# Latent attention on one core: joining and scaling the outputs of two head groups by transfers instead of vector transposes

## Chip, core and metric

The kernel runs on one core of a Trainium2 chip. A core has a matrix engine (TensorE, PE in the profile, with its weight loads as PEld), a vector engine (VectorE, DVE), an engine for functions of one operand (ScalarE, ACT), a general engine (GpSimd, POOL) and a queue engine (SyncE, SP) that issues most of the memory transfers (DMAs). Each works through its own instructions in order and they meet at semaphores. The metric is device time in microseconds for one launch; lower is better. Three runs of the kernel before gave 3230.88, 3235.45 and 3238.08 us, so the time before is their median, 3235.45 us.

## What is computed

The input is x, 8 batches of 1024 tokens of 256 numbers in float32. Two residual blocks follow each other: a latent attention, and two layers of local attention with an MLP. The change touches only the first. Cut to what matters:

```
x = x + attn(layernorm(x))                 # the part touched
x = x + two_local_layers(layernorm(x))

attn(x):                                   # 16 heads of 16, causal
    c_kv   = x @ W_kv_down
    k_rope = rotary(c_kv @ W_k_rope);  q_rope = rotary(x @ W_q_rope)
    k = c_kv @ W_k_up;  v = c_kv @ W_v_up;  q = x @ W_q
    scores = (q.k per head + q_rope.k_rope shared) / sqrt(48)
    w = softmax(causal(scores))
    return concat_heads(w @ v) @ W_o
```

## The kernel before

The first part, `mla`, works batch by batch; the second, `local`, follows when all are done. What is told here is `mla`.

**Units and steps.** Keys lie on the 128 partitions and queries run along the free dimension, so a tile of scores is transposed and its exponentials can go straight into the product with v. The 16 heads form four groups `g` of four, the 1024 queries two halves `c` of 512, the keys eight blocks `kb` of 128. A batch is a list of 36 units, made in the loop over `c in (1, 0)` and `g in (0, 2)`: the second half first, two groups at a time, and within such a pair of groups all key blocks, those above the diagonal left out and the short ones joined so that a unit is always 512 columns wide. So units 0 to 12 belong to groups 0 and 1 of half 1, units 13 to 25 to groups 2 and 3 of half 1, units 26 to 30 to groups 0 and 1 of half 0, and units 31 to 35 to groups 2 and 3 of half 0. A pair of groups is called by its half and its number below, (1,0), (1,1), (0,0) and (0,1).

One unit is handled in one step of a software pipeline three steps deep. In step s, `scores` forms the scores of unit s on PE (two tiles of two PSUM banks) and their exponentials on ACT; `turned` multiplies unit s-1's exponentials, two tiles `pt` of 128x1024, on DVE with the exponentials of the rotary scores `er`, which all heads share; `values` multiplies unit s-2's product with v on PE into an accumulator `acc` of one PSUM bank per group. The values of the last two units of a pair of groups are thus formed two steps after the unit, in the steps given in the section on the change.

**The row sums.** A head's v has 17 columns in memory: its 16 and one of ones. `values` takes 32 columns per head as weights, so of the 32 output partitions that a head has in `acc`, the first 16 are its output, the next one is the sum of its softmax row, and the rest is of no use.

**Normalising and joining.** The output product wants the outputs divided by their row sums and wants two groups side by side, 8 heads of 16 on 128 partitions. When a group's last unit is done, ACT copies `acc` to `oaT` (line 503). One step later `finished` (line 507) lets DVE transpose it in blocks of 32x32, so that the tokens come to the partitions and the row sums to a column, forms the reciprocals, and multiplies 16 of each 32 columns into the tile of the even group. One step later still `turn_back` (line 522) transposes the joined tile back once for each pair of groups, into `oT`. The list at the end of each step (lines 654 to 661) carries this.

**Filler.** The projections, rotary scores, normalisations and output products of this batch, the one before and the next are laid beside the steps by a table written out by hand (lines 554 to 591): `(step, which batch, method, arguments)`, where -1 is the batch before and 1 the next. `out_add` forms two tiles of 128 tokens of the output product in a PSUM bank `psx`; the addition to x and the DMA to memory (`x2d`) are owed, and are paid in the middle of the next step's `turned` by `settle`. PSUM has eight banks: four for scores, two for `acc`, and two that all filler shares (`bank`).

**Order.** For PE, DVE, ACT and POOL the order of instructions is that of the program (`manual_schedule`, line 624). SyncE's issues are placed by the framework. It issues the loads of x, the stores of `x2d`, and the placements of q and k: `place_q` and `place_k` copy each freshly made half of q and k from partition order by heads to the layout that `scores` reads. The last batch has no next one: from step 18 on it runs without filler, its own output products are held back to the end, and the first loads and table scalings of `local` come in beside it. After it the loop runs 11 more steps for what is owed.

Of the kernel before, what the change touches and what calls it, by code (L numbers as in the profile page):

```python
# [29 lines left out]
F32 = mybir.dt.float32  # L30
# [52 lines left out]
def preln_mla_local_kernel(  # L83
# [72 lines left out]
    def mla(ctx: ExitStack, verdict):  # L156
# [94 lines left out]

        ers = [late.tile([P, 1280 + 2048 * c], F32, name=f"er{c}") for c in range(2)]

        norms = wp.tile([P, B], F32, name="norms")
        ones = wp.tile([P, 32], F32, name="ones_m")
        nc.gpsimd.memset(ones, 1.0)
# [9 lines left out]
        class Batch:  # L266
# [177 lines left out]

            def start(self):
                b = self.b
                self.rs = small.tile([P, 2, 4, 16], F32, tag="rs", name=f"rs{b}")
                self.acc, self.onat, self.oTs, self.adds = {}, {}, {}, {}

            def scores(self, key, parts):  # L450

# [34 lines left out]
            def values(self, parts, pts):  # L486

                lo, ended = 0, []
                for c, g, kb in parts:
                    q0, w, _ = self.block(c, kb)  # L490
                    if kb == 0:
                        self.acc[g] = pacc.tile([P, 512], F32, tag=f"acc{g % 2}", name=f"acc{self.b}_{c}_{g}")
                    for n in range(4):
                        h = 4 * g + n
                        nc.tensor.matmul(  # L495
                            self.acc[g][32 * n : 32 * n + 32, q0 - c * 512 :],
                            self.v[:, kb, h * VW : h * VW + 32], pts[n // 2][:, n % 2, lo : lo + w],
                            start=(kb == 0), stop=(kb == 4 * c + 3),
                        )
# [7 lines left out]
            def finished(self, c, g, oT):  # L507


                nat = late.tile([P, 16, 32], F32, tag="onat", name=f"onat{self.b}_{c}_{g}", bufs=2)  # L510
                nc.vector.transpose(nat.rearrange("p b d -> p (b d)"), oT)
                r = self.rs[:, c, g]
                nc.vector.reciprocal(r, nat[:, :, HD])
                e = g % 2
                if e == 0:
                    self.onat[c, g // 2] = nat
                nc.vector.tensor_tensor(
                    self.onat[c, g // 2][:, :, HD * e : HD * e + HD], nat[:, :, :HD],
                    r.unsqueeze(2).to_broadcast([P, 16, HD]), ALU.mult,
                )  # L520

            def turn_back(self, c, g):
                if g % 2:
                    t = late.tile([P, 512], F32, tag="oT", name=f"oT{self.b}_{c}_{g}", bufs=3)
                    nc.vector.transpose(t, self.onat.pop((c, g // 2)).rearrange("p b d -> p (b d)"))
                    self.oTs[c, g // 2] = t
                if (c, g) == (0, 3):
                    verdict(self.rs.rearrange("p c g b -> p (c g b)"), f"a{self.b}")

            def out_add(self, t, i, c=None):  # L530

# [20 lines left out]
            beside.setdefault(step, []).append((who, name, args))  # L552

        for step, who, *what in (
            (0, -1, "out_add", 6, 1, 1), (0, 0, "query", 1, 1, 0),
            (1, 0, "query", 1, 1, 1),
            (2, 0, "value", 2), (2, 0, "low"),
            (3, 0, "keys", 1, 0), (3, 1, "normalise", 0, 0),
            (4, 0, "query", 0, 0, 0), (4, 0, "low"), (4, 1, "normalise", 0, 1), (4, 1, "statistics", 1, 0),
            (5, 0, "query", 0, 0, 1), (5, 1, "normalise", 0, 2), (5, 1, "statistics", 1, 1),  # L560
            (6, -1, "out_add", 0, 0), (6, -1, "out_add", 0, 1), (6, 0, "low"), (6, 1, "normalise", 0, 3),
            (7, 0, "query", 1, 0, 0), (7, 1, "normalise", 1, 0),
            (8, 0, "query", 1, 0, 1), (8, 1, "normalise", 1, 1),
            (9, 0, "value", 3), (9, 0, "low"), (9, 1, "normalise", 1, 2),
            (10, -1, "out_add", 2, 0), (10, -1, "out_add", 2, 1), (10, 1, "normalise", 1, 3),
            (11, 0, "keys", 1, 1),
            (12, 1, "turn", 0, 0), (12, 0, "low"),
            (13, 0, "rotary", 0, 2), (13, 1, "turn", 0, 1),
            (14, 1, "down", 0, 0), (14, 0, "rotary", 0, 3),
            (15, 1, "down", 0, 1), (15, 1, "turn", 1, 0),  # L570
            (16, 0, "rotary", 0, 0), (16, 1, "turn", 1, 1),
            (17, 1, "down", 1, 0), (17, 0, "rotary", 0, 1),
            (18, 1, "down", 1, 1), (18, 1, "rope_q", 0, 0, 0),
            (19, 1, "rope_q", 0, 0, 1), (19, 1, "rope_q", 0, 1),
            (20, 1, "rope_k", 0), (20, 1, "rope_q", 1, 0, 0), (20, 2, "load"),
            (21, 1, "rope_q", 1, 0, 1), (21, 1, "rope_q", 1, 1),
            (22, 1, "rope_k", 1), (22, 1, "query", 0, 1, 0),
            (23, 1, "query", 0, 1, 1), (23, 1, "squares", 0),
            (24, 1, "value", 0), (24, 1, "low"), (24, 1, "squares", 1), (24, 2, "statistics", 0, 0),
            (25, 1, "keys", 0, 0), (25, 2, "statistics", 0, 1),  # L580
            (26, 1, "value", 1), (26, 1, "low"),
            (27, 1, "keys", 0, 1), (27, 1, "rotary", 1, 7),
            (28, 1, "rotary", 1, 0), (28, 1, "low"),
            (29, 1, "rotary", 1, 1), (29, 1, "rotary", 1, 6),
            (30, 1, "reach"),
            (31, 0, "out_add", 4, 0), (31, 0, "out_add", 4, 1),
            (32, 1, "rotary", 1, 3),
            (33, 1, "rotary", 1, 2),
            (34, 1, "rotary", 1, 4), (34, 1, "rotary", 1, 5),
            (35, 0, "out_add", 6, 0), (35, 0, "out_add", 6, 1, 0),  # L590
        ):
            at(step, who, *what)

# [29 lines left out]
        line, done, turning = [], [], []  # L623
        with tc.manual_schedule(engines={E.PE, E.DVE, E.Activation, E.Pool}):
            for b in range(B + 1):
                for step in range(len(units) if b < B else 11):
# [36 lines left out]
        ok = small.tile([P, B], F32, tag="okr", name="okr", bufs=1)  # L663
        nc.vector.tensor_scalar(ok, norms, math.log(TURN) / SCALE, None, ALU.is_le)
# [1242 lines left out]
```

## Time and profile before

One profiled execution took 3236.72 us; its span, first to last instruction, was 3235.0 us. Tables are in us.

| what | value |
|---|---|
| median of three runs | 3235.45 |
| profiled execution | 3236.72 |
| its span | 3235.0 |
| PE busy in the span | 3152.4 (97%) |
| DVE busy | 2654.7 (82%) |
| ACT busy | 1734.6 (54%) |
| POOL busy | 1357.5 (42%) |
| granted PE clock, mean | 0.993 |

A share over the whole span says little, since the two parts have different limits. By stretches of the span the same profile has:

| stretch, us | PE busy | DVE busy | ACT busy | DMA share |
|---|---|---|---|---|
| 400 to 520 (`mla`) | 119.19 of 120 | 114.24 | 105.36 | 0.33 |
| 880 to 1000 (end of `mla`, start of `local`) | 91.34 of 120 | 96.17 | 49.25 | 0.35 |
| 1200 to 3235 (`local`) | 2020.13 of 2035 | 1586.38 | 862.15 | 0.47 |

The profile is read with three kinds of lines. A window line gives the busy time of each engine in a stretch. A line of the chain of waits gives start, length and work of one piece of the chain that ended last, followed back from release to release: time saved in a piece of the chain can shorten the run, time saved elsewhere only makes an idle engine idler. A line of a group gives, for one kind of instruction, its source line, engine, operands, count, busy time and mean length, and behind the last bar the idle time before it. PE's instructions overlap and their ends are modelled, so a busy PE is not a proof that PE sets the pace.

### The profile page before, as it was taken

To read this page: it belongs to the slowest core of one execution; us is meant where nothing else is said; L and a number is where in the kernel's file an instruction comes from. 1 tells how busy PE (TensorE), PEld (TensorE's weight loads), DVE (VectorE), ACT (ScalarE), POOL (GpSimd) and SP (SyncE) were. 2 spreads that over 40 slices of the span, in tenths; PEclk is the share of its full clock that TensorE was granted. 3 is DMA by queue.
4 is the path that set the end of the run, shared out by engine and by line. 5 is a ranking of instruction groups with operands and counts; after the bars stand their busy time and mean duration, and the time that the engine had idled before them with its cause. 6 is when DMAs were issued, how large, how long until landed. Compare 5 with 4: busy or idle time off the path is not lost.

```text
span 3235.0 us, 112699 instructions
## 1 busy us (share of the span) xinstructions
PE 3152.4 (97%) x50210; PEld 1459.7 (45%) x50210; DVE 2654.7 (82%) x3934; ACT 1734.6 (54%) x2183; POOL 1357.5 (42%) x1065
## 2 busy tenths in 40 slices
PE   7999999999977999999999999999999999999998
PEld 2434443444333454444444444445444445444454
DVE  4999999999987888787888877787878788787773
ACT  6888888888742434444444444443444444444441
POOL 1111110100027655555655654555555565555540
PEclk9999999999998999999999999999999999999999
DMA  4133222422433354544545456455544545454431
GB/s 134 43 94 85 64 72 77 105 53 66 118 96 104 108 131 124 136 111 127 125 120 132 114 131 158 120 139 139 147 124 130 131 126 138 129 148 122 118 108 55
DMA packets 389901, 364.21 MB, mean 113 GB/s; under 512 B 158703, under 2 KB 337310, under 8 KB 389278
## 3 DMA queue, kind: packets, MB, share of 16 engines
q1 hardware_dynamic: 387422, 354.51, 41.2%
q8 instruction: 396, 6.49, 0.8%
q10 hardware_dynamic: 1984, 2.41, 0.2%
q14 instruction: 99, 0.81, 0.1%
HBM read 165.96 MB, written 140.51 MB: 95 GB/s over the span
## 4 chain that ended last, share of the span: by engine, by line
PE 83%; DVE 11%; DMA 2%; ACT 1%; SPq 1%; issue 1%; POOL 1%; DVEq 0%; ACTq 0%
PE ag L685 18%; PE pair L685 13%; PE psy L685 9%; PE psw L685 6%; DVE pt L483 6%; PE pv L685 6%; PE o L1018 6%; PE acc L495 6%; PE pair L977 5%; PE sc L461 4%; PE s L1026 2%; PE psR L201 1%; PE psq L201 1%; PE psc L201 1%; PE psrq L201 1%; ACT pt L469 1%
## 5 line engine op out<-in xcount | busy, mean ns | idle before, releaser
L483 DVE TENSOR_TENSOR pt<-pt,er 128x1024 f32<-128x1024 f32 x576 | 677.3, 1220 | 36.9 <-ACT pt L469 35.6
L685 PE MATMUL ag<-d,l 128*32 128x512 f32 x5632 | 639.1, 593 | 2.1 <-DVE xs L1058 1.7
L921 POOL TENSOR_TENSOR t<-t,t 128x1024 f32<-128x1024 f32 x128 | 304.4, 2378 | 798.2 <-DVE t L917 798.2
L469 ACT ACTIVATE pt<-sc 128x1024 f32<-128x1024 f32 x576 | 561.8, 1035 | 93.8 <-PE sc L461 83.7
L983 ACT ACTIVATE pt<-pair 128x1024 f32<-128x1024 f32 (+1 forms) x256 | 235.3, 969 | 540.0 <-PE pair L977 487.3
L685 PE MATMUL pair<-l_qkv,xT 128*32 128x512 f32 x4096 | 468.2, 598 | 3.3 <-DMA xT<-zx 2.5
L126 POOL TENSOR_TENSOR rn<-ss,half 128x16 f32<-128x16 f32 x128 | 373.2, 2915 | 13.8
L685 PEld LDWEIGHTS ag<-d,l 128*32 128x32 f32 x5632 | 176.7, 110 | 375.3 <-issue 354.7
L495 PE MATMUL acc<-pt,v 128*32 128x512 f32 (+3 forms) x3072 | 337.3, 496 | 7.1 <-DVE pt L483 6.9
L912 ACT ACTIVATE sq<-pair 128x1024 f32<-128x1024 f32 x128 | 131.3, 1026 | 350.8 <-issue 301.0
L685 PE MATMUL psy<-l,hid 128*32 128x256 f32 x5120 | 282.1, 379 | 0.0
L685 PEld LDWEIGHTS pair<-l_qkv,xT 128*32 128x32 f32 x4096 | 130.6, 111 | 305.3 <-issue 279.1
L914 DVE TENSOR_TENSOR t<-pair,l_cos 128x1024 f32<-128x1024 f32 x128 | 156.0, 1219 | 122.8 <-ACT sq L912 122.6
L461 PE MATMUL sc<-q,k 32*128 32x512 f32 (+3 forms) x3072 | 247.4, 381 | 8.4 <-ACT pt L469 8.2
L927 POOL TENSOR_TENSOR t<-t,rn 128x1024 f32<-128x1024 f32 x128 | 243.7, 1904 | 10.0
L426 POOL TENSOR_SCALAR_AFFINE_SELECT er<-er 128x128 f32<-128x128 f32 x64 | 45.4, 714 | 478.9 <-ACT er L424 478.9
L1018 PEld LDWEIGHTS o<-pt,v 128*32 128x32 f32 x7680 | 214.6, 110 | 68.3 <-issue 52.9
L1150 DVE SCALAR_TENSOR_TENSOR hid<-ag,l_b,ge 128x512 f32<-128x512 f32 x160 | 116.7, 730 | 155.5 <-ACT ge L1149 86.7
L685 PE MATMUL pv<-l_qkv,xT 128*32 128x512 f32 x2048 | 243.2, 592 | 0.0
L1018 PE MATMUL o<-pt,v 128*32 128x128 f32 x7680 | 233.9, 273 | 3.1 <-POOL pt L985 2.8
L1036 DVE RECIPROCAL rs<-s 128x256 f32<-128x256 f32 x128 | 223.1, 1743 | 16.5 <-PE s L1026 16.4
L685 PE MATMUL psw<-l_o,oT 128*32 128x256 f32 x4096 | 234.7, 381 | 0.7 <-DVE xs L1187 0.7
(326 smaller groups left out, 4594.4 us busy)
## 6 DMA issues: line engine op xcount, KB each, us to landing
z<-turned SPq DMA_DIRECT2D x512, 128.0 KB, 2.4
qkT<-z SPq DMA_DIRECT2D x128, 512.0 KB, 3.5
y<-xs SPq DMA_DIRECT2D x128, 128.0 KB, 3.1
h<-y SPq DMA_DIRECT2D x32, 512.0 KB, 4.4
zx<-turneds SPq DMA_DIRECT2D x120, 128.0 KB, 3.2
xT<-zx SPq DMA_DIRECT2D x240, 64.0 KB, 3.1
zh<-turnedh SPq DMA_DIRECT2D x120, 128.0 KB, 2.4
d<-zh SPq DMA_DIRECT2D x30, 512.0 KB, 3.4
```

The lines of the kernel that those rows point to most:

```text
L126: nc.gpsimd.tensor_tensor(out_, in_, half[:, :n], ALU.pow)
L461: nc.tensor.matmul(two[n // 2][:, n % 2, lo : lo + w], k[rows], q[rows, h], start=(h == 1), stop=(h == 0),)
L469: nc.scalar.activation(pt, sc, AF.Exp, scale=SCALE)
L483: nc.vector.tensor_tensor(t, t, er.to_broadcast([P, 1024 // w, w]), ALU.mult)
L495: nc.tensor.matmul(self.acc[g][32 * n : 32 * n + 32, q0 - c * 512 :], self.v[:, kb, h * VW : h * VW + 32], pts[n // 2][:, n % 2, lo : lo + w],
L685: nc.tensor.matmul(out[four], w[:, four], rhs, start=start, stop=stop)
L921: nc.gpsimd.tensor_tensor(t1, t1, t2, ALU.add)
L927: nc.gpsimd.tensor_tensor(t1, t1, rn.unsqueeze(3).to_broadcast([P, 2, HEADS, DH]), ALU.mult)
L977: nc.tensor.matmul(flat[keys, 2 * j + c, q0:q1].rearrange("p (b t) -> p b t", t=32), qkT[rows, at, t, 1, 2 * g + c, :], q[rows, q0 // 32 : ...
L983: nc.scalar.activation(pt[:, :, : n * P], flat[:, :, : n * P], AF.Exp, scale=-1.0)
L1018: nc.tensor.matmul(o[32 * j : 32 * j + 32, g, a, :], vs[m][:, h * DH + a * 32 : h * DH + a * 32 + 32], pts[m][g][:, place(j), off : off + ...
L1036: nc.vector.reciprocal(rs, s)
```

## The change

In the full batches a group's outputs no longer go through DVE transposes. The weights of an odd group (`g` = 1, 3) begin 16 columns earlier, so that in each 32 partitions of its `acc` the output lies in the last 16 and the row sum, from the column of ones of the head before, in the one ahead of them. `ended` copies `acc` with ACT as before, the even group into the tile `oT` that the output product reads and the odd one into a tile of its own. Then come transfers on SyncE, all of the kind SBUF to SBUF: each of the four row sums of a group is spread over 32 partitions of `rs` (both groups, 8 transfers for a pair), and the four 16-partition strips of the odd group's outputs are laid into the even group's tile (4 transfers).

Three steps after the odd group has ended, `inverse` forms the reciprocals of all row sums of the pair in one instruction of 128x32, writes them to memory (1 transfer), and reads each head's 512 factors back, repeated on the 16 partitions of the head, into a tile `by` (8 transfers). Seven steps after the odd group has ended, `scaled` multiplies the joined tile with `by`. The queue `due` counts these steps.

The pairs are complete in these steps: (1,0) ends in steps 13 and 14, so that `inverse` comes at the end of step 17 and `scaled` at the end of step 21; (1,1) ends in 26 and 27, with 30 and 34; (0,0) in 31 and 32, with 35 and step 3 of the next batch; (0,1) in steps 0 and 1 of the next batch, with 4 and 8.

The output products come later: those of tiles 0 and 2 go from steps 6 and 10 of the next batch to 10 and 11, those of tile 4 from step 31 to 35, and those of tile 6 from steps 35 and 0 to 0 and 1. Other filler moves up to fill the gaps: queries, values and keys in steps 6 to 9, and rotary products in steps 12 and 13 and 31 to 34. The first half of the last batch isn't done by transfers: `straight` transposes `acc` from PSUM with DVE, in the step in which the group ends, and then does as the kernel before did; no copy by ACT is made for it. The loop runs 12 steps after the last batch.

The diff, its new methods whole and the table cut:

```diff
+        zrs = [dram.tile([2, 4, 32, 16], F32, tag=f"zr{i}", name=f"zr{i}") for i in range(2)]
...
-                self.rs = small.tile([P, 2, 4, 16], F32, tag="rs", name=f"rs{b}")
+                self.rs = small.tile([P, 2, 2, 2, 16], F32, tag="rs", name=f"rs{b}")
...
+                    at = HD * (g % 2)
                     for n in range(4):
                         h = 4 * g + n
                         nc.tensor.matmul(
                             self.acc[g][32 * n : 32 * n + 32, q0 - c * 512 :],
-                            self.v[:, kb, h * VW : h * VW + 32], pts[n // 2][:, n % 2, lo : lo + w],
+                            self.v[:, kb, h * VW - at : h * VW - at + 32], pts[n // 2][:, n % 2, lo : lo + w],
...
                     if kb == 4 * c + 3:
-                        oT = late.tile([P, 512], F32, tag="oaT", name=f"oaT{self.b}_{c}_{g}", bufs=2)
-                        on_a(oT, self.acc.pop(g))
-                        ended.append((c, g, oT))
+                        if (self.b, c) != (B - 1, 0):
+                            self.ended(c, g)
+                        ended.append((c, g))
...
+            def ended(self, c, g):
                 e = g % 2
+                if e:
+                    t = late.tile([P, 512], F32, tag="odd", name=f"odd{self.b}_{c}_{g}")
+                else:
+                    t = late.tile([P, 512], F32, tag="oT", name=f"oT{self.b}_{c}_{g}", bufs=4)
+                    self.oTs[c, g // 2] = t
+                on_a(t, self.acc.pop(g))
+                for n in range(4):
+                    row = 32 * n + HD - e
+                    nc.sync.dma_start(
+                        self.rs[32 * n : 32 * n + 32, c, g // 2, e], t[row : row + 1].rearrange("o (p f) -> o p f", f=16)
+                    )
+                if e:
+                    for n in range(4):
+                        rows = slice(32 * n + HD, 32 * n + 32)
+                        nc.sync.dma_start(self.oTs[c, g // 2][rows], t[rows])
+
+            def inverse(self, c, m):
+                r = self.rs[:, c, m]
+                nc.vector.reciprocal(r, r)
+                z = zrs[m]
+                nc.sync.dma_start(z.rearrange("e n p f -> (n p) e f"), r)
+                t = self.by[c, m] = late.tile([P, 512], F32, tag="by", name=f"by{self.b}_{c}_{m}", bufs=2)
+                for n in range(4):
+                    for e in range(2):
+                        lo = 32 * n + HD * e
+                        nc.sync.dma_start(
+                            t[lo : lo + HD], z[e, n].rearrange("p f -> (p f)").partition_broadcast(HD)
+                        )
+                if (c, m) == (0, 1):
+                    verdict(self.rs.rearrange("p c m e f -> p (c m e f)"), f"a{self.b}")
+
+            def straight(self, g):
+                e = g % 2
+                t = late.tile([P, 16, 32], F32, tag=("by", "odd")[e], name=f"nat{g}", bufs=2 - e)
+                nc.vector.transpose(t.rearrange("p b d -> p (b d)"), self.acc.pop(g))
+                r = self.rs[:, 0, g // 2, e]
+                nc.vector.reciprocal(r, t[:, :, HD - e])
+                own = slice(HD * e, HD * e + HD)
                 if e == 0:
-                    self.onat[c, g // 2] = nat
+                    self.by[0, g // 2] = t
+                both = self.by[0, g // 2]
                 nc.vector.tensor_tensor(
+                    both[:, :, own], t[:, :, own], r.unsqueeze(2).to_broadcast([P, 16, HD]), ALU.mult
                 )
+                if e:
+                    u = self.oTs[0, g // 2] = late.tile([P, 512], F32, tag="oT", name=f"oTs{g}", bufs=4)
+                    nc.vector.transpose(u, both.rearrange("p b d -> p (b d)"))
...
+            def scaled(self, c, m):
+                t = self.oTs[c, m]
+                nc.vector.tensor_tensor(t, t, self.by.pop((c, m)), ALU.mult)
...
-            (0, -1, "out_add", 6, 1, 1), (0, 0, "query", 1, 1, 0),
-            (1, 0, "query", 1, 1, 1),
+            (0, -1, "out_add", 6, 0), (0, 0, "query", 1, 1, 0),
+            (1, -1, "out_add", 6, 1), (1, 0, "query", 1, 1, 1),
...
-            (6, -1, "out_add", 0, 0), (6, -1, "out_add", 0, 1), (6, 0, "low"), (6, 1, "normalise", 0, 3),
-            (7, 0, "query", 1, 0, 0), (7, 1, "normalise", 1, 0),
-            (8, 0, "query", 1, 0, 1), (8, 1, "normalise", 1, 1),
-            (9, 0, "value", 3), (9, 0, "low"), (9, 1, "normalise", 1, 2),
-            (10, -1, "out_add", 2, 0), (10, -1, "out_add", 2, 1), (10, 1, "normalise", 1, 3),
-            (11, 0, "keys", 1, 1),
-            (12, 1, "turn", 0, 0), (12, 0, "low"),
+            (6, 0, "query", 1, 0, 0), (6, 0, "low"), (6, 1, "normalise", 0, 3),
+            (7, 0, "query", 1, 0, 1), (7, 1, "normalise", 1, 0),
+            (8, 0, "value", 3), (8, 0, "low"), (8, 1, "normalise", 1, 1),
+            (9, 0, "keys", 1, 1), (9, 1, "normalise", 1, 2),
+            (10, -1, "out_add", 0, 0), (10, -1, "out_add", 0, 1), (10, 0, "low"), (10, 1, "normalise", 1, 3),
+            (11, -1, "out_add", 2, 0), (11, -1, "out_add", 2, 1),
+            (12, 1, "turn", 0, 0), (12, 0, "rotary", 0, 2),
...
-            (31, 0, "out_add", 4, 0), (31, 0, "out_add", 4, 1),
+            (31, 1, "rotary", 1, 2),
             (32, 1, "rotary", 1, 3),
-            (33, 1, "rotary", 1, 2),
-            (34, 1, "rotary", 1, 4), (34, 1, "rotary", 1, 5),
-            (35, 0, "out_add", 6, 0), (35, 0, "out_add", 6, 1, 0),
+            (33, 1, "rotary", 1, 4),
+            (34, 1, "rotary", 1, 5),
+            (35, 0, "out_add", 4, 0), (35, 0, "out_add", 4, 1),
...
-                    if turning:
-                        bt, e = turning.pop(0)
-                        bt.turn_back(*e)
-                    if done:
-                        bt, e = done.pop(0)
-                        bt.finished(*e)
-                        turning.append((bt, e[:2]))
-                    done += ended
+                    for what in due:
+                        what[0] -= 1
+                    while due and due[0][0] == 0:
+                        due.pop(0)[1]()
+                    for bt, (c, g) in ended:
+                        if (bt.b, c) == (B - 1, 0):
+                            bt.straight(g)
+                        elif g % 2:
+                            due.append([3, lambda bt=bt, c=c, g=g: bt.inverse(c, g // 2)])
+                            due.append([7, lambda bt=bt, c=c, g=g: bt.scaled(c, g // 2)])
+                            due.sort(key=lambda what: what[0])
```

More of the change, by code (lines that the diff above doesn't have):

```diff
@@ L446, in start @@
                 b = self.b
-                self.rs = small.tile([P, 2, 4, 16], F32, tag="rs", name=f"rs{b}")
-                self.acc, self.onat, self.oTs, self.adds = {}, {}, {}, {}
+                self.rs = small.tile([P, 2, 2, 2, 16], F32, tag="rs", name=f"rs{b}")
+                self.acc, self.by, self.oTs, self.adds = {}, {}, {}, {}
             def scores(self, key, parts):
@@ L501, in values @@
                     if kb == 4 * c + 3:
-                        oT = late.tile([P, 512], F32, tag="oaT", name=f"oaT{self.b}_{c}_{g}", bufs=2)
-                        on_a(oT, self.acc.pop(g))
-                        ended.append((c, g, oT))
-                return ended
[L507 to L513, printed above, removed]
-                e = g % 2
+                        if (self.b, c) != (B - 1, 0):
+                            self.ended(c, g)
@@ L517, in finished @@
                 nc.vector.tensor_tensor(
-                    self.onat[c, g // 2][:, :, HD * e : HD * e + HD], nat[:, :, :HD],
-                    r.unsqueeze(2).to_broadcast([P, 16, HD]), ALU.mult,
-                )
[L522 to L528, printed above, removed]
+                    both[:, :, own], t[:, :, own], r.unsqueeze(2).to_broadcast([P, 16, HD]), ALU.mult
+                )
@@ L530, in out_add @@
+                if e:
+                    u = self.oTs[0, g // 2] = late.tile([P, 512], F32, tag="oT", name=f"oTs{g}", bufs=4)
+                    nc.vector.transpose(u, both.rearrange("p b d -> p (b d)"))
+                if g == 3:
+                    verdict(self.rs.rearrange("p c m e f -> p (c m e f)"), f"a{self.b}")
+            def scaled(self, c, m):
+                t = self.oTs[c, m]
+                nc.vector.tensor_tensor(t, t, self.by.pop((c, m)), ALU.mult)
             def out_add(self, t, i, c=None):
@@ L560, in mla @@
             (5, 0, "query", 0, 0, 1), (5, 1, "normalise", 0, 2), (5, 1, "statistics", 1, 1),
-            (6, -1, "out_add", 0, 0), (6, -1, "out_add", 0, 1), (6, 0, "low"), (6, 1, "normalise", 0, 3),
-            (7, 0, "query", 1, 0, 0), (7, 1, "normalise", 1, 0),
-            (8, 0, "query", 1, 0, 1), (8, 1, "normalise", 1, 1),
-            (9, 0, "value", 3), (9, 0, "low"), (9, 1, "normalise", 1, 2),
-            (10, -1, "out_add", 2, 0), (10, -1, "out_add", 2, 1), (10, 1, "normalise", 1, 3),
-            (11, 0, "keys", 1, 1),
-            (12, 1, "turn", 0, 0), (12, 0, "low"),
-            (13, 0, "rotary", 0, 2), (13, 1, "turn", 0, 1),
-            (14, 1, "down", 0, 0), (14, 0, "rotary", 0, 3),
+            (6, 0, "query", 1, 0, 0), (6, 0, "low"), (6, 1, "normalise", 0, 3),
[5 more added lines that the diff above has]
+            (12, 1, "turn", 0, 0), (12, 0, "rotary", 0, 2),
+            (13, 1, "turn", 0, 1), (13, 0, "rotary", 0, 3),
+            (14, 1, "down", 0, 0),
             (15, 1, "down", 0, 1), (15, 1, "turn", 1, 0),
@@ L622, in mla @@
         E = mybir.EngineType
-        line, done, turning = [], [], []
+        line, due = [], []
         with tc.manual_schedule(engines={E.PE, E.DVE, E.Activation, E.Pool}):
             for b in range(B + 1):
-                for step in range(len(units) if b < B else 11):
+                for step in range(len(units) if b < B else 12):
                     if b == B - 1 and step == ALONE:
```

## The prediction

> **What bounds the kernel now.** I read the busy table by windows first, one batch of the first layer and one stretch of it, then the chain of waits inside that batch, then the groups by shape, then SyncE's issues. The windows (length; busy us of PE, its weight loads, DVE, ACT, POOL; clock, DMA share, GB/s):
>
> ```profile
> 540.00:650.81 110.81, 110.02 (x1284) 45.75 (x1280) 106.09 (x131) 96.63 (x129) 11.63 (x14) 1.00 0.30 77
> 581.30:621.60 40.30, 40.11 (x461) 16.68 (x461) 39.92 (x56) 33.79 (x46) 4.30 (x5) 1.00 0.21 53
> ```
>
> A batch comes every 110.81 us (the same pieces of the chain return at 360.37, 471.18 and 581.99). PE looks full everywhere, but its ends are modelled; the chain decides. Columns: start, us, piece:
>
> ```profile
> 581.99 3.40 DVE pt L483 x3
> 585.39 0.60 DVE x L542
> 585.99 1.13 DVE pt L483
> 587.13 0.63 DVE onat L511
> ...
> 587.78 0.27 DVE rs L513
> ...
> 588.07 0.42 DVE onat L517
> 588.49 2.27 DVE pt L483 x2
> ...
> 594.40 0.62 DVE oT L525
> ...
> 622.65 0.67 PE sc L461 x7
> 623.32 0.99 PE acc L495 x8
> 624.32 0.86 PE psq L201 x8
> ```
>
> From 581.3 (step 31 of 36) to 621.6 (step 7 of the next batch) the chain never leaves DVE; in the other 70 us it is nearly all PE. Four of the eight normalisations of a batch fall into that stretch, and they stand on the chain themselves. That is where the change can earn; elsewhere DVE's work lies beside PE's.
>
> The removed instructions of one batch (busy us, mean ns), and prices for a transfer (SyncE's time to issue so many; the last line: median from issue to landing):
>
> ```profile
> L511 DVE STREAM_TRANSPOSE onat<-oaT 128x512 f32<-128x512 f32 x8 | 5.6, 702 | 0.0
> L517 DVE TENSOR_TENSOR onat<-onat,rs 128x256 f32<-128x256 f32 x8 | 3.4, 425 | 0.3
> L525 DVE STREAM_TRANSPOSE oT<-onat 128x512 f32<-128x512 f32 x4 | 2.8, 703 | 0.0
> L513 DVE RECIPROCAL rs<-onat 128x16 f32<-128x16 f32 x8 | 2.0, 253 | 0.3
> 606.22 3.07 SPq L376 DMA_DIRECT2D q<-alves_place_q(1, 1)_7500  x4
> 10.80 2.18 SPq L226 DMA_DIRECT2D wout<-in_L_attn_W_o_dram  x5
> x2d<-x SPq DMA_DIRECT2D x32, 256.0 KB, 2.4
> ```
>
> **DVE.** Removed per batch: 5.6 + 3.4 + 2.8 + 2.0 = 13.8 us. Added: four reciprocals of 128x32 and four products of 128x512. The product is nearest to L542, 684 ns for 128x512. The reciprocal lies between L513 (253 ns for 16 elements) and twice that; I take 350 ns, with both ends for the range (0.6 us a batch, hidden or not). So 4 x 1.03 = 4.1 us added, 9.7 saved a batch.
> In the stretch: four groups at 0.63 + 0.27 + 0.42 = 1.32, two turn-backs at 0.62, and 0.2 of gaps, together 6.7 us leave the chain. What comes in is two reciprocals (steps 35 and 4) and two products (steps 34 and 3), 2.1 us. One add of L542 (0.6) moves behind the stretch. DVE there goes from 39.9 to about 34.7.
>
> **PE takes over.** The number of matmuls is the same: an odd group's weights begin 16 columns earlier, with the same 32 columns. PE's price of a step, from the chain: 0.7 + 1.0 for scores and values, plus the filler (0.86 a dense product of 512 columns, 0.43 a low part, 1.73 a pair of output products). The filler of steps 31 to 6 is 14.9 us, so twelve steps cost 12 x 1.7 + 14.9 = 35.3 us. The stretch can fall by at most 40.3 - 35.3 = 5.0 us. The output products that leave step 6 for steps 10 and 11 cost the same 1.73 there, where PE sets the pace.
> But ACT is busy 33.8 of these 40.3 us and none of that work goes: three engines at 34 to 35 us in strict step with each other don't reach 35.3. The new order also puts the four rotary products, each with an exponential on ACT (0.6 us), into steps 31 to 34 and the PE-heavy output products into 35, 0 and 1, so ACT's and PE's busy steps no longer alternate as well. Between 0 and 5.0 I take 3.0 per stretch: at 634 to 646 us ACT is at 11.83 of 12.20 with the chain on PE, so PE can hold its pace at such a load, though not always. Seven stretches (they start near 138, 249, ... 803): **-21 us**.
>
> **A bank.** The products for tile 6 now keep their PSUM bank until the add in step 2, where `value 2` wants one. PE reaches it 1.7 us into the step; DVE's first product and the add take 1.22 + 0.68 = 1.9. Some 0.4 us with latency, at 0 if DVE runs early, at 1.1 as the longest wait of `psq` for L542 shows: 7 x 0.4 = **+2.8**.
>
> **Transfers.** Each pair of groups issues 4 + 4 row sums, 4 rows of the odd group, 1 to memory and 8 back: 21 on SyncE's queue, 84 a batch, beside 38 now. At 2.18 / 5 = 0.44 us each that is 37 us more of 110; SyncE is mostly idle now. What hides them is the steps left for them, so the budgets matter. Three steps for the sums: 12 issues (5.3) and a landing (2.4) = 7.7, while steps 32 to 34 take about 7.7 and steps 2 to 4 about 8.5. Four steps from reciprocal to product: 0.44 + 2.4 (to memory) + 8 x 0.44 + 2.4 (back) = 8.8 us. PE's price of the steps between: 35 to 2, 13.3; 4 to 7, 11.1; 30 to 33, 10.3; 17 to 20, 12.0. All fit, with 1.5 to 4.5 us left. If late, DVE stands at L483's neighbour and behind it the next products of `pt` wait, and PE's `acc` for them. Also queued behind these issues: the placements of q and k. They have time: q for group 2 is placed in step 2 and first read in step 13. The output products wait for the scaled tile two steps after it (8 to 10) or one (34 to 35). I take no stall in the seven full batches. The copies of `acc` on ACT stay (8 a batch); the added memory traffic, 8 x 32 KB a pair and little else, is small beside 0.30 DMA share.
>
> The Trainium skill speaks against this part: DMA: Bandwidth & Descriptors, Rules for kernel authors, says to coalesce small transfers, as under 64 KB one pays mostly overhead, and not to split a load by partition halves; all 84 are under 64 KB, and eight of each pair fill one tile. Its Anatomy section puts the fixed part at about 2.0 us, mostly the receipt of the write; the row shows 2.4 to landing, and with 2.0 the chain would be 8.0 rather than 8.8, an estimate from that page. Rule and budget agree only as long as the issue, not the landing, is what repeats.
>
> **The last batch.** From 871 us no filler is left and DVE sets the pace: 66.86 of the 73 us to 944. The first-half pairs lose 3.5 us of DVE work each and get 1.0: one pair counts in full, the other for about half, -3.7. The second half transposes straight from PSUM, the same instructions as now; reading PSUM costs L542 684 ns against 702 for L511, so nothing; four copies of 0.62 leave ACT, idle there. Against it: around 872 a 1.5 MB weight load and small ones go out (8.01 us of the chain is `l_fcos` behind it), in the very steps in which pair (1,0) fetches its factors. I take 2.2 us of DVE stall, between 0 and 8: **-1.5**.
>
> **Sum.** The profiled execution took 3236.7 (span 3235.0), 1.3 over the median of 3235.45: 3236.7 - 21 + 2.8 - 1.5 = **3217**. The two-layer second part, 2290 us, is untouched.
>
> **Rivals.**
> (B) Another engine had DVE's stretch covered: ACT and the worse mix of steps hold it at 40, the gain is 0 to 1 per stretch, 3230 to 3240, say 3235. For: ACT at 84% there and the rotary products bunched. Against: ACT idles 4.2 us in the stretch waiting for PE's scores.
> (C) Slower: the factors of pair (0,1) come late. One place, steps 4 to 8, and its neighbours. If an issue costs 0.77 (3.07 / 4, the row of q) instead of 0.44, the chain is 11.7 against 11.1 and 10.3; and if the four issues of q stand ahead of the one to memory, 3.07 more. Late by 0.6 + 1.4 + 3.07 = 5.1 a batch, less the 2.6 won: 3236.7 + 7 x 2.5, about 3254 (the last batch taken as even). It decides from 0.7 us an issue, or 2.3 us of queue in front. For: steps 0 to 4 ask SyncE for 21 new issues besides 8 placements. Against: small issues at 0.44, a mostly idle queue.
> (D) PE's floor is reached: 7 x 5.0 - 2.8 + 1.5, 3203. For: PE held its pace beside ACT at 97%. Against: three engines near 35.
>
> **How the numbers follow.** Forecast 0.50 (own range 3205 to 3229), B 0.17, C 0.27, D 0.06. About 0.2% (6.5 us) is what a measurement of this kernel can tell from no change. Faster: forecast and D, 0.56; same: B, 0.17; slower: C, 0.27. The range runs from D to C's middle, 3202 to 3256; it leaves out the upper half of C and the edge of D, 0.16.
>
> **What would show it.** The chain at steps 31 to 7 should be PE pieces instead of DVE ones, with DVE near 96 us a batch and the period near 108.2. If the period is unchanged and ACT's `pt` stands in the chain, B. If the chain shows DMA of the factors or sums with DVE idle before the new product or reciprocal, C; idle there of over 3 us a batch makes the prediction wrong. A stall of PE before `psv` in step 2 prices the bank; DVE idle around 870 to 885 the last batch.

## The result and the profile after

Six runs of the changed kernel had a median of 3281.89 us (3279.88 to 3287.54); six of the kernel before on the same chip 3235.11. The ratio is 1.0148, 95% interval 1.0135 to 1.0161: slower by 1.5%, where 0.6% faster was forecast, and beyond the end of the range (3256). One execution of one version below (e8) ran at a granted clock of 0.60 and took 5395 us; it is set aside, and why it did so stays open.

The two profiles, with spans of 3235.0 and 3280.5 us, place the loss. A batch begins with its first product of scores; `mla` ends with the start of its last output product.

| piece, us | before | after | difference |
|---|---|---|---|
| start to the second batch | 153.5 | 152.0 | -1.5 |
| six batches, second to seventh | 665.3 (110.9 each) | 708.2 (118.0 each) | +42.9 |
| last batch with its tail | 121.4 | 126.2 | +4.8 |
| second part | 2294.7 | 2294.1 | -0.6 |

So the answer lies in a full batch. Where in it? I measured each step from its first product of scores to the next one's, in the fifth batch of each kernel, and do so for the experiments too (their columns are used below):

| steps of the fifth batch, us | before | after | new order only | one transfer for four sums | no transfers |
|---|---|---|---|---|---|
| 31 to 35 and 0 to 7 | 41.42 | 46.21 | 40.53 | 38.30 | 38.27 |
| 8 to 12 | 14.46 | 16.59 | 16.56 | 16.58 | 16.58 |
| 13 to 30 | 54.93 | 54.60 | 54.59 | 54.58 | 54.58 |
| batch | 110.81 | 117.40 | 111.67 | 109.47 | 109.43 |

The windows of the kernel after, the sixth batch and then three stretches inside it, from its step 6 on (length; busy us of PE, its weight loads, DVE, ACT, POOL; clock, DMA share, GB/s):

```profile
624.70:742.60 117.90, 112.45 (x1284) 45.38 (x1280) 97.49 (x110) 96.62 (x128) 13.15 (x14) 0.97 0.35 87
643.43:651.70 8.27, 3.67 (x22) 1.01 (x20) 4.90 (x9) 2.97 (x5) 2.38 (x3) 0.96 0.74 180
651.70:658.52 6.82, 6.82 (x38) 1.92 (x42) 4.39 (x5) 4.70 (x7) 0.00 (x0) 0.54 0.60 136
658.52:665.00 6.48, 6.22 (x77) 2.46 (x73) 4.72 (x4) 6.39 (x11) 0.00 (x0) 1.00 0.63 139
```

DVE got its relief (97.49 against 106.09 in a batch). In 8.27 us from 643.43, called the hole below, no engine is busy for much more than half of the time, and PE only for 3.67. Then PE works 6.82 us at a granted clock of 0.54, and only after that at full clock again. The first 1000 us hold 61 us at half clock, against 24 in the kernel before. What the engines wait for in the hole stands in the chain of waits (start, us, piece):

```profile
641.86 0.86 PE psq L201 x8
642.72 0.70 PE sc L462 x4
...
643.65 4.85 DMA q<-alves_place_q(1, 1)_7777
...
648.73 0.07 ACT alves_place_q(0, 0)_7930 L79
...
650.62 1.03 ACT pt L470
...
651.70 1.22 PE sc L462 x6
652.92 1.86 PE acc L497 x8
```

From 604.9 to 643.4 every piece of this chain is PE's: DVE has left it, as forecast. Then comes a transfer of q, `place_q(1,1)`, and what waits for it is not a reader of q: it is ACT's copy of the next half but one, `place_q(0,0)`. ACT's line (the bracket holds the idle time before it, and its cause):

```profile
634.61 0.59 ACT L79 CAST alves_place_q(1, 1)_7777<-psq 128x512 fp32r<-128x512 f32 x1
...
648.73 0.59 ACT L79 CAST alves_place_q(0, 0)_7930<-psq 128x512 fp32r<-128x512 f32 x1 [5.90 <-DMA q<-alves_place_q(1, 1)_7777]
```

The copies go into the tile `halves` (line 356), which has two buffers. The copy after next must wait until the transfer has read the buffer out. That buffer was full at 635.2; the transfer had landed at 648.5. SyncE's issues show why (start, us for so many):

```profile
632.54 2.43 SPq L523 DMA_DIRECT2D rs<-oT  x4
635.07 2.44 SPq L523 DMA_DIRECT2D rs<-odd  x4
637.56 3.51 SPq L529 DMA_DIRECT2D oT<-odd  x4
641.17 0.53 SPq L584 DMA_DIRECT2D x2d<-x  x1
641.79 3.12 SPq L377 DMA_DIRECT2D q<-alves_place_q(1, 1)_7777  x4
645.01 3.48 SPq L392 DMA_DIRECT2D k<-alves_place_k(1, 0)_7846  x4
648.58 0.55 SPq L535 DMA_DIRECT2D zr<-rs  x1
650.61 3.57 SPq L540 DMA_DIRECT2D by<-zr  x8
```

The queue goes from one group to the next without a pause. Row sums and strips of pair (0,1) stand ahead of q, which begins 6.6 us after its half was ready. Only between the write to memory and the first read back is there a gap, 1.5 us here, and there the queue stands: the read back waits for the write, and everything else behind it. From 600.0 to 657.4 SyncE issues 82 transfers in 48.7 us; with the 0.05 us that the trace shows between two, and three such gaps (4.1), that is 56.9 of the 57.4. A stretch of that length in the kernel before has 26 issues and 17.2 us.

In the fifth batch the hole and what follows it are steps 6 and 7, of 8.35 and 5.26 us; the version with fewer transfers has 3.19 and 2.55 there. That is 5.2 of standing and 2.7 of slow clock, together 7.9, and the first table's columns differ by just that (117.40 and 109.47).

### The profile page after: what moved, and what is told of

It reads as the page before. It is cut to its first block, busy times and chain, and to the rows that moved or that the text cites. A ratio compares the mean times of both kernels' runs of the same rounds, so it can differ in the third digit from the quotient of the medians.

```text
span 3280.5 us, 113619 instructions
## 1 busy us (share of the span) xinstructions
PE 3167.7 (97%) x50210; PEld 1461.2 (45%) x50210; DVE 2591.5 (79%) x3784; ACT 1730.6 (53%) x2179; POOL 1364.1 (42%) x1065
## 4 chain that ended last, share of the span: by engine, by line
PE 88%; DVE 4%; DMA 3%; ACT 2%; SPq 1%; issue 1%; POOL 0%; ACTq 0%; DVEq 0%
PE ag L729 18%; PE pair L729 13%; PE psy L729 9%; PE acc L497 8%; PE psw L729 6%; PE sc L462 6%; PE pv L729 6%; PE o L1062 6%; PE pair L1021 5%; PE psR L201 2%; PE s L1070 2%; PE psq L201 2%; ACT pt L470 1%; PE psx L201 1%; PE psc L201 1%
## 5 line engine op out<-in xcount | busy, mean ns | idle before, releaser
L497 PE MATMUL acc<-pt,v 128*32 128x512 f32 (+3 forms) x3072 | 328.2, 505 | 5.2 <-DVE pt L484 4.8
L462 PE MATMUL sc<-q,k 32*128 32x512 f32 (+3 forms) x3072 | 260.7, 389 | 16.7 <-ACT pt L470 15.6
L427 POOL TENSOR_SCALAR_AFFINE_SELECT er<-er 128x128 f32<-128x128 f32 x64 | 58.4, 915 | 521.0 <-ACT er L425 472.1
```

Source lines behind the costliest of these rows:

```text
L462: nc.tensor.matmul(two[n // 2][:, n % 2, lo : lo + w], k[rows], q[rows, h], start=(h == 1), stop=(h == 0),)
L497: nc.tensor.matmul(self.acc[g][32 * n : 32 * n + 32, q0 - c * 512 :], self.v[:, kb, h * VW - at : h * VW - at + 32], pts[n // 2][:, n % 2, ...
```

## The experiments

All were timed beside the kernel before on their chip; the ratios are to it. Theory Q: SyncE's queue is full across the batch's end, so the halves of q are read out late, and ACT, then PE, then PE's clock pay for it. Its main rivals: the factors come late to DVE's product; the order of the filler is worse; the traffic itself costs.

**A third buffer (e1).**

```diff
-                 t = p1.tile([P, 2, 512], F32R, tag="halves", ..., bufs=2)
+                 t = p1.tile([P, 2, 512], F32R, tag="halves", ..., bufs=3)
-                t = self.by[c, m] = late.tile([P, 512], F32, tag="by", ..., bufs=2)
+                t = self.by[c, m] = late.tile([P, 512], F32, tag="by", ...)
```

(`rs` gets one buffer, made with the first pair, and `straight` keeps its even tile in a buffer of `xn`, for room.)

> The changed kernel with three buffers instead of two for the halves tile between ACT's copies and the placements of q and k (the factors' tile and the row sums' tile go down to one buffer to make room). Theory Q (SyncE's queue is full, the placement of q(1,1) goes out 7 us late, and ACT stands 5.9 us at the next copy but one because the halves have only two buffers; PE then idles and its clock is halved for 6.8 us): steps 6 and 7 lose their excess of 5.9 and 2.9 us, about 7.9 a batch over the usual 0.7, seven times: 3282 - 55 = about 3227, 3218 to 3240, period 109 to 110. Theory M (the new order of the filler costs the time, the transfers are innocent): 3282, unchanged. Theory F (the factors come late and DVE waits for them before the product): 3282, unchanged.

Measured: 3275.43 us, ratio 1.0117 (1.0101 to 1.0134). A miss for Q as I had put it. The trace has no wait of ACT for `halves` any more, and steps 0 to 7 take 23.84 us (31.62 in the changed kernel, 23.71 in the version of the next section). But the hole has moved to step 10. Its wait (total, times, longest) and its chain:

```profile
DVE oT L572 <- DMA by<-zr: 7.1, 1, 7.1
```

```profile
517.34 1.97 DMA zr<-rs
...
522.01 1.70 SPq L540
...
523.75 2.05 DMA by<-zr
```

DVE stands 7.1 us at the product of pair (0,1), as the queue is late with the write and the eight reads. This is rival C's waiter: it is there, but second in line behind the same full queue. Taking away one waiter only uncovered the next. Nor is the total a fair measure of e1: its `mla` ends 32 us earlier than that of the changed kernel (954.2 against 986.4), and its second part takes 2316 us instead of 2294. More on this stands with e6 below.

**One transfer for the four row sums of a group (e2): 15 issues a pair instead of 21.** The bytes are the same.

```diff
-                for n in range(4):
-                    row = 32 * n + HD - e
-                    nc.sync.dma_start(
-                        self.rs[32 * n : 32 * n + 32, c, g // 2, e], t[row : row + 1].rearrange("o (p f) -> o p f", f=16)
-                    )
+                nc.sync.dma_start(
+                    self.rs[:, c, g // 2, e], t[HD - e : P : 32].rearrange("n (p f) -> n p f", f=16)
+                )
```

> The changed kernel with the four row sums of a group in one transfer instead of four: 15 issues a pair instead of 21. Theory Q: 6 x 0.63 = 3.8 us less queue for each of the two pairs that stand ahead of q(1,1), 7.6 us in all against 7 us of delay, so the stall of ACT goes or shrinks to 1 us: 3225 to 3240. Theory M: 3282. Theory F: the factors come 3.8 us earlier too, so most of the loss would go as well, but then DVE's idle time before the product must have been the cause in the changed kernel's trace.

Measured: 3229.28 us, ratio 0.9967 (0.9957 to 0.9978): faster than the kernel before. A window of one batch, and SyncE around the same place:

```profile
590.50:700.10 109.60, 108.70 (x1284) 44.58 (x1280) 97.32 (x110) 96.31 (x128) 15.19 (x14) 1.00 0.38 94
```

```profile
597.15 0.58 SPq L521 DMA_DIRECT2D rs<-odd  x1
597.85 2.46 SPq L527 DMA_DIRECT2D oT<-odd  x4
600.41 0.53 SPq L582 DMA_DIRECT2D x2d<-x  x1
601.08 3.08 SPq L377 DMA_DIRECT2D q<-alves_place_q(1, 1)_7657  x4
```

A transfer of four sums is issued in the time of one, and q goes out at 601.08, 0.02 us after its half is done. The clock is 1.00 throughout the batch.

**The same 21 transfers, eight of them issued by GpSimd (e5).**

```diff
-                    nc.sync.dma_start(
+                    nc.gpsimd.dma_start(
                         self.rs[32 * n : 32 * n + 32, c, g // 2, e], t[row : row + 1].rearrange("o (p f) -> o p f", f=16)
```

> The changed kernel with the eight row-sum transfers of a pair issued by POOL instead of SyncE; their number, size and path through the transfer engines stay. Theory Q (what is short is SyncE's time to issue, 0.63 us each): as with one transfer per group, 3225 to 3240, the stall of ACT gone or below 1.5 us. Theory T (the transfer engines or the landing of 64-byte pieces are short, whoever issues): 3275 to 3290, unchanged.

Measured: 3229.15 us, ratio 0.9980 (0.9970 to 0.9989), period 109.5. Neither bytes nor number of transfers changed, only who issues them, and the whole loss is gone. So it was SyncE's issue time and its order, not the load on the transfer engines.

**The transfers laid beside the kernel before (e3 and e12).** The normalising by DVE stays; row sums, strips (of 128 columns) and factors (of 256) are moved and not read. e3 has 21 issues a pair, e12 has 15, by the edit of e2.

```diff
+            def more(self, c, g, oT):
...
+                for n in range(4):
+                    row = 32 * n + HD
+                    nc.sync.dma_start(
+                        self.spare[32 * n : 32 * n + 32, e], oT[row : row + 1].rearrange("o (p f) -> o p f", f=16)
+                    )
...
+                        nc.sync.dma_start(strips[rows], oT[rows, :128])
```

> The kernel before, with the new transfers issued beside it in the same places (row sums, strips, to memory, factors; strips and factors with shorter rows so that they fit), their results never read. DVE's work and the order of the filler stay as they were. Theory Q: the placement of q(1,1) is late again, ACT stands for it, and the clock falls: 5 to 8 us in each of seven batches, 3270 to 3291. Theory M and theory F: 3235, as before.

> The kernel before with the new transfers laid beside it and their results not read, the row sums of a group in one transfer: 15 issues a pair instead of the 21 that took it to 3285. A dose test. If SyncE's time for the issues is the cause, and it acts once the queue fails to run empty before the placements of q, most of the loss goes at once: 3236 to 3248, with a period of 110.8 to 111.5. If the traffic or any extra transfer costs in proportion, the loss falls to 15/21 of 49 us: about 3270, with a period near 115.

Measured: e3 3285.08 us, ratio 1.0138 (1.0121 to 1.0155); e12 3237.79 us, 1.0004 (0.9995 to 1.0013). The transfers alone make the kernel before as slow as the change does, with the same wait in each batch from the second on (5.2 to 7.5 us):

```profile
529.04 0.58 ACT L79 CAST alves_place_q(0, 0)_6623<-psq 128x512 fp32r<-128x512 f32 x1 [7.46 <-DMA q<-alves_place_q(1, 1)_6464]
```

Of the 52.3 us between the two profiles, 36.9 lie in the six full batches; the last batch with its tail has 9.5 and the second part 6.9, and the start is 0.9 shorter.

And six issues fewer take away all of it, not six parts in 21. This is not because the queue runs empty, as I had expected. In e12 too a write to memory and the first read back stand ahead of `place_q(1,1)`, whose half is ready at 605.9, and ACT waits:

```profile
608.66 3.08 SPq L377 DMA_DIRECT2D q<-alves_place_q(1, 1)_7852  x4
```

```profile
615.97 0.59 ACT L79 CAST alves_place_q(0, 0)_8011<-psq 128x512 fp32r<-128x512 f32 x1 [1.55 <-DMA q<-alves_place_q(1, 1)_7852]
```

In the second to eighth batch of e12, q goes out 2.8 to 3.8 us late and ACT stands 1.1 to 2.7 us, at no cost that the total shows. In the changed kernel and in e3 q is 5.6 to 9.0 us late and ACT stands 5.0 to 7.5 us. From the first issue of this q to ACT's copy it is 7.3 us here and 6.9 in the changed kernel, so the landing is not what differs. With these two doses the cost looks like a threshold: a delay within the slack of ACT and PE is hidden, and one beyond it costs 3 to 8 us a batch (e3's period is 113.9 to 118.7).

**The new order alone (e4).** The kernel before with the changed table of filler, as in the diff of the change, and its 12 closing steps.

```diff
-            (6, -1, "out_add", 0, 0), (6, -1, "out_add", 0, 1), (6, 0, "low"), (6, 1, "normalise", 0, 3),
+            (6, 0, "query", 1, 0, 0), (6, 0, "low"), (6, 1, "normalise", 0, 3),
...
+            (10, -1, "out_add", 0, 0), (10, -1, "out_add", 0, 1), (10, 0, "low"), (10, 1, "normalise", 1, 3),
+            (11, -1, "out_add", 2, 0), (11, -1, "out_add", 2, 1),
...
-                for step in range(len(units) if b < B else 11):
+                for step in range(len(units) if b < B else 12):
```

> The kernel before with the changed kernel's table of filler and nothing else: DVE transposes and normalises as before, no new transfers. Theory Q: within 10 us of before, 3225 to 3245. Theory M: most of the 46 us, 3270 to 3290.

Measured: 3244.04 us, ratio 1.0016 (1.0007 to 1.0026), period 111.67, against 110.81. The order costs 0.86 us a batch by itself. The table of steps says where: the stretch gains 0.9, steps 8 to 12 lose 2.1, and 13 to 30 gain 0.3.

**Without the transfers (e13).** This version leaves its outputs neither joined nor divided and serves for its time alone.

```diff
-                for n in range(4):
-                    row = 32 * n + HD - e
...
-                            due.append([3, lambda bt=bt, c=c, g=g: bt.inverse(c, g // 2)])
-                            due.append([7, lambda bt=bt, c=c, g=g: bt.scaled(c, g // 2)])
```

> The changed kernel without row sums, strips, reciprocals, factors and scaling in the full pairs: its outputs there are neither joined nor divided. It gives the floor of a batch. If PE and ACT hold the period once the queue is out of the way, it stays at 109.2 to 109.5, as in the version with 15 issues a pair, and the whole stands at 3222 to 3232 unless the second part runs otherwise on these values. If DVE's four reciprocals and products (4.1 us a batch) or the 60 issues still cost, it is 108.5 or lower.

Measured: 3226.20 us, ratio 0.9967 (0.9954 to 0.9981). Its batch:

```profile
589.20:698.60 109.40, 108.43 (x1284) 44.40 (x1280) 93.72 (x99) 96.23 (x128) 11.97 (x14) 1.00 0.30 78
```

DVE has another 3.6 us less to do than in e2 and the period is the same, 109.45. So neither DVE nor the queue holds the period of the new order any more. PE is busy for 108.43 of it, and from 598.6 to 636.9 its pieces make up all of the chain but 0.6 us; that PE sets the floor is read from this and not tested.

**Further cuts of the queue (e6, e8, e9, e10, e11).** e6 is e2 with the third buffer of e1; e8 is e6 with pair (1,0) of the last batch normalised by DVE from PSUM; e9 is e8 with the reciprocals out in four transfers and back in one, 11 issues a pair; e10 is e2 with these 11 issues; e11 is e2 with that pair by DVE. The edits of the factors and of the pair:

```diff
+                    nc.sync.dma_start(z[n].rearrange("e p f -> p e f"), r[32 * n : 32 * n + 32])
...
+                nc.sync.dma_start(
+                    t, z.rearrange("n e p f -> (n e) (p f)").unsqueeze(1).to_broadcast([8, HD, 512])
+                )
...
+            def by_dve(self, c, g):
+                return self.b == B - 1 and (c == 0 or g < 2)
```

> One transfer per group for the row sums and three buffers for the halves, together. Theory Q: what is left of ACT's wait for the placement of q(1,1) goes, 0.3 to 1 us a batch off the period of 109.5: 3222 to 3228. If the period stays at 109.5, PE and the mix of the filler hold it now and not the queue: 3227 to 3232.

> As the run with both, and in the last batch the first pair (1,0) is transposed straight by DVE too, so that nothing waits for its factors behind the first weight loads of the second part. If those waits cost time (l_cos and the factors stand with 7.8 and 3.8 us in the chain near 863 to 875): 3 to 6 us less than the run with both. If DVE's added work (3.5 us less 1.0) eats it: the same within 2 us.

> As the one before, and the reciprocals go to memory in four transfers and come back in one of 128 partitions: 5 issues a pair instead of 9, 11 in all instead of 21. Theory Q without any queue left in the way: the same within 2 us. If the queue still costs something: 2 to 5 us less. If one 256 KB load from memory comes later than eight of 32 KB: DVE idle before the product, and slower.

> The changed kernel with the four row sums of a group in one transfer, and the reciprocals out in four transfers and back in one that fills all 128 partitions, instead of one out and eight back: 11 issues a pair of groups in place of 21. No buffer is added. The theory (SyncE's queue, then the buffer that ACT waits for) has nothing left to take after the version with 15 issues: its batch period of 109.5 should stay within 0.2, and the time at 3225 to 3233. The rival (the factors still come late to DVE's product) expects a shorter period, under 109.2, and under 3225 us. A period over 110 would say that four transfers to memory ahead of the one back are slower than one ahead of eight.

> The changed kernel with the row sums of a group in one transfer, and in the last batch also pair (1,0) normalised by DVE straight from PSUM, as the first half of that batch is. The seven full batches should keep their period of 109.5. If the last batch loses because its factors come late behind the loads of the next part, it gets 2 to 5 us shorter than the 119.7 of the version with one transfer for the sums, and the time is 3224 to 3228. If it doesn't, that loss is not the factors', and the time stays at 3228 to 3231 or rises by the DVE work that comes back (some 2 us).

| version | us | ratio (interval) | period |
|---|---|---|---|
| e6 | 3236.05 | 1.0004 (0.9995 to 1.0013) | 109.44 to 109.49 |
| e8 | 3237.94 | 1.0008 (0.9998 to 1.0017) | 109.44 to 109.47 |
| e9 | 3238.01 | 1.0010 (1.0001 to 1.0019) | 109.44 to 109.48 |
| e10 | 3231.50 | 0.9981 (0.9972 to 0.9990) | 109.43 to 110.03 |
| e11 | 3230.99 | 0.9977 (0.9967 to 0.9987) | 109.43 to 110.56 |

None gets a batch below 109.4, as e13 says. e8 and e9 stay within 2 us of e6, as one reading of each expectation had it. e6 was a miss in time: with it `mla` ends 13 us earlier than with e2 (last output product at 916.2 against 929.6), and the second part takes that and more back, 2318 us instead of 2297; after the end of `mla` its chain has 16.57 us without a wait that the trace shows, and then weight loads that come late. e1, e6, e8 and e9 share the edit of the buffers, and with it another layout of the tiles in memory, and all four have this longer second part (2316 to 2320 us). It isn't the early end of `mla`, since e1's ends later than that of the kernel before (954.2 against 940.2). I take the layout for the cause, but no run separates it from the rest of that edit. e10 lost 5.5 us in its tail against e2 (125.2 and 119.7): in the last batch's chain its one wide transfer of factors takes 11.27 us to land, beside the loads for the second part, where e2's chain has 3.75.

e11 shortens nothing: its last batch takes 121.0, so late factors cost that batch of e2 no more than the DVE work that replaces them (some 2 us by the estimate made before the run).

## Why the prediction was wrong

**The step that failed** is in its part on transfers: "Also queued behind these issues: the placements of q and k. They have time: q for group 2 is placed in step 2 and first read in step 13", and with it "I take no stall in the seven full batches". I looked for the reader of the placed q, and it does have time. The one who has none is the writer of the buffer that the transfer empties: ACT, three steps on, with two buffers. It stood 5.0 to 7.1 us a batch where the prediction had put nothing, and with the slow clock behind it this made the fifth batch 7.9 us longer. e3 shows that wait without any of the other edits, e1 removes it by a third buffer, and e2 and e5 remove its cause.

**What made the queue late** were two numbers. An issue was priced at 0.44 us. In the six full batches the reads of the factors did cost 0.43, but the row sums and strips 0.63 and the placements 0.74; the 84 new ones come to 46 us a batch instead of 37. Larger was the other: "SyncE is mostly idle now" was read over a whole batch. Three of the four pairs and five of the eight placements fall between step 27 and step 7, the 57 us shown above. There the new issues took 34 us and the old ones 15, and no sum was made for this stretch. At my own price it would have come to 61 x 0.44 + 14.1 for the placements + 0.9 for the stores + 8 of gaps = 50 of 57 us: not full, yet close enough that a burst had to be late.

**What was right.** The relief of DVE (8.6 us a batch by the windows; 9.7 forecast), with both new instructions at the prices taken (350 and 684 ns), and PE taking over the stretch. The groups of the changed kernel, with the idle time before them:

```profile
L533 DVE RECIPROCAL rs<-rs 128x32 f32<-128x32 f32 x30 | 10.5, 349 | 19.6 <-DMA rs<-odd 14.4 <-DMA oT<-odd 5.0 <-issue 0.2
L569 DVE TENSOR_TENSOR oT<-oT,by 128x512 f32<-128x512 f32 x30 | 20.6, 686 | 1.7 <-DMA by<-zr 1.2 <-DMA rs<-oT 0.2
```

Even the first line shows the full queue: DVE stood 19.6 us in all for sums and strips that three steps were to hide. The factors cost nearly nothing here, since the hole before them gives them time. Without the queue's cost (e2) the stretch goes from 41.42 to 38.30: 3.1, where 3.0 was forecast. e4 and e2 divide this: 0.9 comes from the order, 2.2 from DVE's relief. Over a whole batch the order costs 0.86 and the relief is worth 2.2.

That 3.0 was met is in part luck, since the 5.0 it was taken from was worked wrongly. The window of 40.30 us ends two thirds through step 7, which runs from 619.64 to 622.58 in the kernel before, but 35.3 prices only the twelve steps 31 to 6, and its 14.9 us of filler are those of the old table. At the same prices steps 31 to 7 of the new table also hold 14.9 us of filler, and thirteen steps cost 13 x 1.7 + 14.9 = 37.0, which is 4.4 under the 41.42 measured over them.

**A second, smaller miss.** The net gain of a batch is 1.3, not 2.6. The wait for the bank (0.4 forecast) is found in e4 alone, where the weight loads of `psv` wait for the add once a batch, 0.8 us at most, and step 2 takes 3.04 us against 2.95 in e2; in the changed kernel and in e2 it isn't there. What was left out are steps 10 and 11. The text said that the output products "cost the same 1.73 there, where PE sets the pace", but the sum has no term for it: steps 8 to 12 grew by 2.1 us. With 3.12 - 2.12 + 0.35 = 1.35 the period of e2 is explained (110.81 - 109.47 = 1.34).

**The last batch**: -1.7 in e2 (119.7 against 121.4), -1.5 forecast. The agreement is partly luck: in e4 the new order alone makes it 1.6 longer (123.0), which the sum had not, so the rest is worth 3.3. The 2.2 of DVE's stall were not measured by themselves. In the changed kernel it is +4.8, as it begins with the same hole.

**The rivals.** C had the right queue and the right place (steps 4 to 8), and 0.63 us an issue is near the 0.7 from which it was to decide; but it named the second waiter, and at 3254 it was far too small, since it knew neither of ACT's buffer nor of the clock. B falls: relief of DVE did shorten the stretch. D falls too: it took 5.0 us off the stretch, and with all of the new work left out (e13) it is 3.2.

The sum afterwards, per batch: +0.86 for the order, -2.2 for DVE's relief, +7.9 for the queue in the fifth batch (8.5 on the mean of six). With the mean, 0.86 - 2.2 + 8.5 = 7.15, and six times that is 42.9.

**Coalescing.** The Trainium skill, DMA: Bandwidth & Descriptors, Rules for kernel authors, asks to coalesce small transfers. Here that was worth 53 us by the medians (3281.9 to 3229.3; 59 by the ratios to the kernel before), though not for the reason of bytes and overhead of each transfer: e5 keeps all the small transfers and gains as much. The same page, Issuing engines are not separate DMA queues, says that spreading issues over engines only saves the sequencer's time, which is usually small beside the transfer. In this kernel that time caused the whole loss.

## What to carry to other kernels

Sum the issues of a queue over the busiest stretch, old ones included and at the price of each kind, and not over a period; a late transfer costs nothing while whoever needs it has slack (2.8 to 3.8 us late was free here), and beyond that it costs at once. For a transfer that is moved behind others, ask who refills its source, not only who reads its destination. When filler leaves a stretch, enter it where it arrives; and when removing one wait brings little, look for the next waiter on the same resource before dropping the theory.

## What the runs showed of the hardware

The time to issue a transfer did not go by its bytes: 0.63 us for a row sum of 2 KB, 0.60 for four of them in one, 0.43 for a read of factors of 32 KB. After 8.3 us in which PE was busy for 3.67, its clock was granted at 0.54 for 6.8 us, and this was a third of the loss of a batch (2.7 of 7.9). The 4.6 us without work were three gaps, the longest of 3.33:

```profile
649.37 0.49 PE L362 MATMUL psq<-alves_place_q(0, 0)_7930,minus 128*128 128x512 f32 x1 [3.33 <-ACT alves_place_q(0, 0)_7930 L79]
```

In the six batches of the changed kernel between 150 and 860 us this gap was 3.0 to 4.3 us, and half clock came behind each. In e3 it came behind gaps of 2.1, 2.5 and 2.7 us too (each with a second one of 0.9 us soon after), and in e1 behind 2.1, 2.2 and 2.9 us; gaps of 1.3 us in e3 and of 1.2 and 1.5 us in e1 left the clock full. The Trainium skill, TensorE: Matmul & The Clock Gate, HAM oscillation, warns of gaps in PE's work of over some 3.4 us. In this kernel shorter ones were enough. The prediction had not weighed this.

The fewest transfers were not the fastest to land in the one place compared, the last batch beside the loads for the second part: 11.27 us for the one of e10 against 3.75 for the last of eight in e2.
